# Attention and a non-local block on one core: a third score block at the start of each attention, the bias of the values in one accumulator slot, an ordered first load with products of zeros ahead of it, and the last chunk of z in halves

## The chip, the cores and the metric

The kernel runs on one core of a Trainium2 chip. The metric is the device time in microseconds (us), from the first to the last instruction of that core; smaller is better. Before the change three runs took 2209.11, 2209.64 and 2211.08 us; the median is 2209.64 us. The profile shown is one execution with a span of 2209.6 us.

The engines are TensorE (PE in the profile; PEld is its loading of weights), VectorE (DVE), ScalarE (ACT), GpSimd (POOL) and SyncE (SP). DMA transfers are issued here from the SP and the ACT queue, and all use the core's 16 DMA engines.

## The reference

Eight images of 512 channels and 32 x 32 positions, float32. Cut to what is computed:

```python
def layer0(x, Wq, bq, Wk, bk, Wv, bv, Wp, bp):          # 8 heads of 64 channels
    q, k, v = conv1x1(x, Wq, bq), conv1x1(x, Wk, bk), conv1x1(x, Wv, bv)
    attn = softmax(einsum('bhdn,bhdm->bhnm', q, k) * 64 ** -0.5)
    return x + conv1x1(einsum('bhnm,bhdm->bhdn', attn, v), Wp, bp)

def layer1(x, g_w, g_b, theta_w, theta_b, phi_w, phi_b, W_w, W_b, gamma, beta):
    g, theta, phi = conv1x1(x, g_w, g_b), conv1x1(x, theta_w, theta_b), conv1x1(x, phi_w, phi_b)
    f = einsum('bcn,bdn->bcd', theta, phi) / n
    z = conv1x1(einsum('bcd,bdn->bcn', f, g), W_w, W_b) + x
    mean, var = z.mean((0, 2, 3)), z.var((0, 2, 3))      # over all eight images
    return (z - mean) * rsqrt(var + 1e-5) * gamma + beta

out = layer1(layer0(x))
```

The normalization at the end needs the statistics of a channel over all eight images, so no output can be stored before the last image's z of that channel is there.

## The kernel before

PSUM, where TensorE writes, is cut into four slots of two banks each. A list `free` holds their names from the one idle longest to the one used last. `next_bank` takes the one idle longest.

```python
    free = ["s0", "s1", "s2", "s3"]

    def bank(tag, name):
        return psum.tile([P, 2, 512], F32, tag=tag, name=name)

    def next_bank(name):
        free.append(free.pop(0))
        return bank(free[-1], name)
```

The large products (q, k, v, the projection, theta and phi, g, z) are each done as seven products of quarter matrices instead of eight. The quarters of a weight are loaded as `w[:, 0]`, `w[:, 1]`, `w[:, 2]` and a corner `a21`; four sums of them, `w[:, 3]` to `w[:, 6]`, are made by VectorE, as are four sums of the quarters of the data (`t1` to `t4`). Three slots take the products; the fourth of the list stands idle during them, and the slot used last goes to the end of the list.

```python
    def weight_sums(w, a21):
        for to, l, r, op in ((3, a21, w[:, 2], ALU.add), (4, w[:, 3], w[:, 0], ALU.subtract),
                             (5, w[:, 0], a21, ALU.subtract), (6, w[:, 1], w[:, 4], ALU.subtract)):
            nc.vector.tensor_tensor(w[:, to], l, r, op)
    ...
    # (name, weight, data, slot, quarters of the result that read the slot after it)
    SEVEN = (("11", 0, "11", 0, (("11", True),)), ("s1t1", 3, "t1", 1, (("22", True),)),
             ("s2t2", 4, "t2", 0, (("12", True),)), ("s4", 6, "22", 1, (("12", False),)),
             ("s3t3", 5, "t3", 0, (("22", False),)), ("12", 1, "21", 2, (("11", False),)),
             ("t4", 2, "t4", 0, (("21", True),)))
    EARLY = (SEVEN[0], SEVEN[5], *SEVEN[1:4], ...)        # the order for q of image 0

    def seven(name, w, data, positions_out, first, add, between=None, early=False):
        nk, half = w.shape[2], w.shape[3]
        tags = list(free)
        free[:] = [tags[3], tags[1], tags[0], tags[2]] if early else [tags[3], tags[1], tags[2], tags[0]]
        ...
            for to_ps, at, lhsT, rhs in parts:
                for k in range(nk):
                    pe(nc.tensor.matmul(to_ps, lhsT(k), rhs(k), start=(s, at) not in begun, stop=(k == nk - 1),
                                        skip_group_check=True))
                    begun.add((s, at))
            for to, is_first in reads:
                (first if is_first else add)(to, ps)
```

The first loads: four of the first weight on the ACT queue, four of the first image on the SP queue, then two small biases and the second weight.

```python
    load_w(nc.scalar)
    for h in range(NH):
        for k in range(2):
            at = slice(k * CC // 2, (k + 1) * CC // 2), slice(h * 512, (h + 1) * 512)
            nc.sync.dma_start(xt[:, at[0], at[1]], x_v[0, :, at[0], at[1]])
    bq, bk = load_col("bq", nc.scalar), load_col("bk", nc.scalar)
    load_w(nc.sync)
    ...
    data = data_sums(quarters_of(xt), "x_0")
    q, peak_q = heads_of(0, "q", weights("WqT"), bq, data, early=True)
```

The attention of one image has 64 steps. A step makes a block of scores in a slot, takes the exponential on ScalarE, and two steps later (`LAG`) multiplies it with the values. Two slots alternate for scores, two for the weighted sums of one unit of eight steps and the next.

```python
        def scores(i):
            u, m = steps[i]
            ps = bank(tags[i % 2], f"ps_{b}_{u}_{m}")
            ...                                            # four matmuls
            e = block(f"e_{b}_{u}_{m}")
            nc.scalar.activation(e, ps, AF.Exp, scale=SCALE)
            ...                                            # sums of e on VectorE

        def weighted(i):
            u, m = steps[i]
            if m == 0:
                sums[u] = bank(tags[2 + u % 2], f"po_{b}_{u}")
            ...                                            # four matmuls, at the end two reads
        ...
        for i in range(len(steps) + LAG):
            if i < len(steps):
                scores(i)
            if i >= LAG:
                weighted(i - LAG)
```

The bias of the values goes through the projection into the projection's bias, once, before the projection of image 0:

```python
    def join_bias(w):
        for oc in range(CC):
            m, mc = divmod(oc, CC // 2)
            ps = next_bank(f"pbp_{oc}")
            for c in range(CC):
                ...
                pe(nc.tensor.matmul(ps[:, 0, :1], quarter[:, kc, mc * P:(mc + 1) * P], bv[:, c:c + 1],
                                    start=(c == 0), stop=(c == CC - 1)))
            nc.vector.tensor_tensor(bp[:, oc:oc + 1], bp[:, oc:oc + 1], ps[:, 0, :1], ALU.add)
```

The end: z of the last three images, one chunk of 128 channels (`oc`) after the other. After the third image of a chunk the statistics of that chunk are joined (`begin`), its factors computed and all eight images of the chunk scaled and stored (`finish`).

```python
    def last_z():
        order = [B - LATE, B - 1, *range(B - LATE + 1, B - 1)]
        begun = None
        for oc in range(CC):
            for n, b in enumerate(order):
                _, g, wf = late[b]
                ps = next_bank(f"pz_{b}_{oc}")
                for h in range(NH):
                    for d in range(IC):
                        pe(nc.tensor.matmul(ps[:, h, :], wf[:, d, oc * P:(oc + 1) * P], g[d][:, h * 512:(h + 1) * 512],
                                            start=(d == 0), stop=(d == IC - 1)))
                t = z[b][oc]
                dve(nc.vector.scalar_tensor_tensor(t, ps.rearrange("p h n -> p (h n)"), wb[:, oc:oc + 1], t,
                                                   ALU.add, ALU.add))
                if n == 0 and begun:
                    finish(oc - 1, *begun)
                for h in range(NH):
                    dve(nc.vector.bn_stats(stats[:, oc, b * NH + h, :], t[:, h * 512:(h + 1) * 512]))
            begun = begin(oc)
        finish(CC - 1, *begun)
```

`pe(...)` and `dve(...)` keep the instructions so marked in the order of the program on their engine; the others may be moved by the scheduler.

Of the kernel before, what the change touches and what calls it, by code (L numbers as in the profile page):

```python
# [8 lines left out]
F32 = mybir.dt.float32  # L9
# [21 lines left out]
def unshifted(ctx: ExitStack, tc: tile.TileContext, a: dict, out: bass.AP):  # L31
# [11 lines left out]
    LATE = 3  # L43
    LAG = 2
# [86 lines left out]
    def weights(name):  # L131

        n, w = loaded.pop(0)
        assert n == name
        if name not in kept:
            weight_sums(w, corner[name])
            kept[name] = dram.tile(list(w.shape), F32, tag=f"kept_{name}", name=f"kept_{name}")
            nc.sync.dma_start(kept[name], w)
        return w

    def join_bias(w):

        for oc in range(CC):
            m, mc = divmod(oc, CC // 2)
            ps = next_bank(f"pbp_{oc}")
            for c in range(CC):
                k, kc = divmod(c, CC // 2)
                quarter = {(0, 0): w[:, 0], (0, 1): w[:, 1], (1, 0): corner["WpT"], (1, 1): w[:, 2]}[m, k]
                pe(nc.tensor.matmul(ps[:, 0, :1], quarter[:, kc, mc * P:(mc + 1) * P], bv[:, c:c + 1],
                                    start=(c == 0), stop=(c == CC - 1)))  # L150
            nc.vector.tensor_tensor(bp[:, oc:oc + 1], bp[:, oc:oc + 1], ps[:, 0, :1], ALU.add)  # L151
# [23 lines left out]
    def seven(name, w, data, positions_out, first, add, between=None, early=False):  # L175
# [7 lines left out]
        for n, (what, wi, di, s, reads) in enumerate(EARLY if early else SEVEN):  # L183
# [11 lines left out]
            for to_ps, at, lhsT, rhs in parts:  # L195
                for k in range(nk):
                    pe(nc.tensor.matmul(to_ps, lhsT(k), rhs(k), start=(s, at) not in begun, stop=(k == nk - 1),  # L197
                                        skip_group_check=True))
                    begun.add((s, at))
# [19 lines left out]
    load_w(nc.scalar)  # L219
    for h in range(NH):  # L220
        for k in range(2):
            at = slice(k * CC // 2, (k + 1) * CC // 2), slice(h * 512, (h + 1) * 512)
            nc.sync.dma_start(xt[:, at[0], at[1]], x_v[0, :, at[0], at[1]])
# [27 lines left out]
    def heads_of(b, what, w, bias, data, **how):  # L251
# [13 lines left out]
        for c in range(CC):  # L265
            nc.vector.tensor_reduce(peak[:, c:c + 1], t[:, c, :], AX.X, ALU.max, apply_absolute_value=True)
# [30 lines left out]
    def attention(b, q, k, v, near_end):  # L297
# [18 lines left out]
        def scores(i):  # L316
            u, m = steps[i]
            p, h = units[u]
            ps = bank(tags[i % 2], f"ps_{b}_{u}_{m}")
# [216 lines left out]
# [3 lines that stand above are left out]
        for oc in range(CC):  # L539
            for n, b in enumerate(order):  # L540
                _, g, wf = late[b]
                ps = next_bank(f"pz_{b}_{oc}")
                for h in range(NH):
                    for d in range(IC):
                        pe(nc.tensor.matmul(ps[:, h, :], wf[:, d, oc * P:(oc + 1) * P], g[d][:, h * 512:(h + 1) * 512],  # L545
                                            start=(d == 0), stop=(d == IC - 1)))
# [320 lines left out]
```

## Time and profile before

| What | Value |
|---|---|
| Time, median of three runs | 2209.64 us |
| Span of the profiled execution | 2209.6 us |
| PE busy | 2166.6 us (98%) |
| DVE busy | 1321.1 us (60%) |
| ACT busy | 735.8 us (33%) |
| First matmul of image 0 | at 6.29 us |
| First score block of image 0 | at 81.7 us |
| Last large matmul ends | at about 2187.5 us |
| First store of the output issued | at 2162.75 us |
| Moved by DMA over the span | 209.07 MB |

How to read the lines: a row of the waits has the engine and line that waited, what it waited for, then the total in us, how often and the longest. A row of the timeline has the start and the length in us, the engine, the line of the kernel, the operation, what is written and what is read, their shapes and how many instructions were merged; in brackets stands the idle time ahead of it and what ended it. One float32 matmul of the program appears as two passes, each with its weight load.

### The profile page before, as it was taken

Reading aid. Unit: us, or ns where it says so; the run is one execution under the profiler, and the core shown is the slowest. Engines: PE = TensorE matmul, PEld = TensorE weight load, DVE = VectorE, ACT = ScalarE, POOL = GpSimd, SP = SyncE. Lnnn points to the kernel's source line nnn. Section 1 sums busy time; section 2 is a strip of 40 time slices with the busy share of each in tenths; the row PEclk is TensorE's granted clock in tenths of the full one; section 3 lists DMA queues with packets and bytes.
Section 4 is the critical chain, followed back from the end, with each engine's and each line's share of the span. In section 5 each row is a group of like instructions: output and inputs, shape, how many; then the busy total and the mean of one; then the engine's idle time right before and its main releaser. Section 6 shows DMA issues by size and latency. Waiting matters only on the chain.

```text
span 2209.6 us, 28905 instructions
## 1 busy us (share of the span) xinstructions
PE 2166.6 (98%) x12234; PEld 1066.1 (48%) x12234; DVE 1321.1 (60%) x1299; ACT 735.8 (33%) x821; POOL 35.4 (2%) x36
## 2 busy tenths in 40 slices
PE   8999999999999999999999999999999999999996
PEld 3534664346633456335563365633655336643362
DVE  5476546765467644776547755467463765447736
ACT  1463103641046310462105621165203641055215
POOL 0000000000000000000000000000000000000000
PEclk9999999999999999999999999999999999999998
DMA  6212323113131232312223113231334113222347
GB/s 238 77 39 60 126 98 120 39 44 133 60 129 39 60 107 75 116 40 69 96 93 105 40 64 119 90 91 31 108 114 143 39 30 129 79 84 66 129 159 306
DMA packets 58265, 209.07 MB, mean 95 GB/s; under 512 B 10384, under 2 KB 16784, under 8 KB 52752
## 3 DMA queue, kind: packets, MB, share of 16 engines
q1 hardware_dynamic: 56752, 206.09, 28.5%
q8 instruction: 98, 1.61, 0.3%
q10 hardware_dynamic: 1376, 1.05, 0.2%
q14 instruction: 39, 0.32, 0.0%
HBM read 129.12 MB, written 46.53 MB: 79 GB/s over the span
## 4 chain that ended last, share of the span: by engine, by line
PE 93%; DMA 3%; DVE 2%; issue 1%; ACT 1%; SPq 0%; DVEq 0%; ACTq 0%
PE ps L324 19%; PE po L346 19%; PE pp L197 9%; PE pq L197 9%; PE ptp L197 9%; PE pv L197 8%; PE pk L197 6%; PE pg L197 4%; PE pf L449 3%; PE pz L197 2%; DMA r<-den_d 2%; PE pz L545 2%; PE pwf L468 1%; PE den L295 1%; ACT e L327 0%
## 5 line engine op out<-in xcount | busy, mean ns | idle before, releaser
L327 ACT ACTIVATE e<-ps 128x1024 f32<-128x1024 f32 x512 | 523.7, 1024 | 390.7 <-PE ps L324 383.1
L333 DVE TENSOR_TENSOR acc<-acc,e 128x1024 f32<-128x1024 f32 x384 | 470.0, 1224 | 123.7 <-ACT e L327 117.1
L324 PE MATMUL ps<-q,k 64*64 64x512 f32 x4096 | 532.4, 591 | 2.6 <-ACT e L327 2.6
L346 PE MATMUL po<-e,v 64*64 64x512 f32 x4096 | 529.5, 590 | 0.0
L324 PEld LDWEIGHTS ps<-q,k 64*64 64x64 f32 x4096 | 155.0, 133 | 291.6 <-issue 278.9
L346 PEld LDWEIGHTS po<-e,v 64*64 64x64 f32 x4096 | 156.7, 133 | 283.9 <-issue 281.2
L458 ACT ACTIVATE g<-pg,gb 128x512 f32<-128x512 f32 x32 | 22.0, 687 | 434.3 <-PE pg L197 434.3
L331 DVE TENSOR_TENSOR acc<-e,e 128x1024 f32<-128x1024 f32 x64 | 78.2, 1223 | 121.0 <-ACT e L327 87.7
L197 PE MATMUL pk<-t_x,w_WkT 128*128 128x512 f32 x256 | 114.0, 593 | 0.7 <-DVE k L214 0.7
L197 PE MATMUL pv<-w_WvT,t_x 128*128 128x256 f32 x512 | 114.5, 379 | 0.0
L197 PE MATMUL ptp<-w_tp,t_x 128*128 128x256 f32 x512 | 114.4, 379 | 0.0
L197 PE MATMUL pp<-t_o,w_WpT 128*128 128x512 f32 x256 | 113.7, 593 | 0.0
L197 PE MATMUL pq<-t_x,w_WqT 128*128 128x512 f32 x256 | 113.6, 592 | 0.0
L197 PEld LDWEIGHTS ptp<-w_tp,t_x 128*128 128x128 f32 x512 | 97.3, 190 | 13.2
L197 PEld LDWEIGHTS pv<-w_WvT,t_x 128*128 128x128 f32 x512 | 97.2, 190 | 13.2
L197 PE MATMUL pq<-x,w_WqT 128*128 128x512 f32 x192 | 89.7, 612 | 6.3 <-DMA w_WqT<-in_WqT_dram 6.3
L262 ACT ACTIVATE k<-pk,bk 128x512 f32<-128x512 f32 x64 | 40.5, 684 | 165.0 <-PE pk L197 165.0
L384 DVE TENSOR_TENSOR o<-o,r 128x512 f32<-128x512 f32 x60 | 40.8, 689 | 91.0 <-DMA r<-den_d 91.0
L197 PE MATMUL pp<-o,w_WpT 128*128 128x512 f32 x192 | 91.1, 620 | 2.2 <-DVE bp L151 2.2
L278 ACT COPY v<-pv 128x1024 f32<-128x1024 f32 x32 | 32.4, 1012 | 173.6 <-PE pv L197 173.6
L262 ACT ACTIVATE q<-pq,bq 128x512 f32<-128x512 f32 x62 | 39.2, 683 | 146.2 <-PE pq L197 146.2
L197 PE MATMUL pv<-w_WvT,x 128*128 128x256 f32 x384 | 87.5, 381 | 0.0
(132 smaller groups left out, 1947.4 us busy)
## 6 DMA issues: line engine op xcount, KB each, us to landing
fold<-acc SPq DMA_DIRECT2D x240, 128.0 KB, 2.3
x<-in_x_dram SPq DMA_DIRECT2D x32, 512.0 KB, 5.5
r<-den_d SPq DMA_DIRECT2D x120, 128.0 KB, 3.0
w_WqT<-kept_WqT SPq DMA_DIRECT2D x7, 1792.0 KB, 7.4
w_WvT<-kept_WvT SPq DMA_DIRECT2D x7, 1792.0 KB, 7.3
w_WkT<-kept_WkT SPq DMA_DIRECT2D x7, 1792.0 KB, 7.1
w_WpT<-kept_WpT SPq DMA_DIRECT2D x7, 1792.0 KB, 8.7
w_tp<-kept_tp SPq DMA_DIRECT2D x7, 1792.0 KB, 7.3
```

Source lines behind the costliest of these rows:

```text
L197: pe(nc.tensor.matmul(to_ps, lhsT(k), rhs(k), start=(s, at) not in begun, stop=(k == nk - 1), skip_group_check=True))
L262: nc.scalar.activation(t[:, c, cols(q)], ps[:, m, :], AF.Identity, bias=bias[:, c:c + 1])
L278: seven(f"pv_{b}", w, data, True, lambda q, ps: nc.scalar.copy(at(q), as_v(ps)), lambda q, ps: nc.vector.tensor_tensor(at(q), at(q), as_v( ...
L295: pe(nc.tensor.matmul(ps[j * D:(j + 1) * D, :], lhsT, rhs(j), start=True, stop=True, skip_group_check=True))
L324: pe(nc.tensor.matmul(ps[c * P // 2:(c + 1) * P // 2, j, :], k[r, p, keys], q[r, p, h * 512:(h + 1) * 512], start=True, stop=True, skip_gr ...
L327: nc.scalar.activation(e, ps, AF.Exp, scale=SCALE)
L331: nc.vector.tensor_tensor(accs[u], es[u, 0], e, ALU.add)
L333: nc.vector.tensor_tensor(accs[u], accs[u], e, ALU.add)
L346: pe(nc.tensor.matmul(ps[j * D:(j + 1) * D, r, :], v[keys, m, (2 * p + j) * D:(2 * p + j + 1) * D], e[keys, j, :], start=(m == 0), stop=(m ...
L384: dve(nc.vector.tensor_tensor(part(4 * g + i), part(4 * g + i), r, ALU.mult))
L449: pe(nc.tensor.matmul(ps[:, c, :], tp[:, i, c * P:(c + 1) * P], tp[:, i, CI:], start=(i == 0), stop=(i == NB - 1)))
L545: pe(nc.tensor.matmul(ps[:, h, :], wf[:, d, oc * P:(oc + 1) * P], g[d][:, h * 512:(h + 1) * 512], start=(d == 0), stop=(d == IC - 1)))
```

## The change

It has four parts. In an attention the third score block (step 2) goes to a slot that is not needed before the second unit, so three blocks can be made before the first exponential is done; the two slots then alternate the other way round. The four columns of the joined bias go into one slot and are added by one instruction. At the start the loads of the first image and of the first weight are issued in pairs, smallest first, eight products of zeros run on TensorE ahead of the first real one, the first product goes through its channels chunk by chunk, and the sums of data and weights are put in one order. The last chunk of z is made, added and counted in halves.

```diff
+    WARM = 8
...
     def join_bias(w):
 
+        ps = next_bank("pbp")[:, 0, :CC]
         for oc in range(CC):
             m, mc = divmod(oc, CC // 2)
-            ps = next_bank(f"pbp_{oc}")
             for c in range(CC):
...
-                pe(nc.tensor.matmul(ps[:, 0, :1], quarter[:, kc, mc * P:(mc + 1) * P], bv[:, c:c + 1],
-                                    start=(c == 0), stop=(c == CC - 1)))
-            nc.vector.tensor_tensor(bp[:, oc:oc + 1], bp[:, oc:oc + 1], ps[:, 0, :1], ALU.add)
+                pe(nc.tensor.matmul(ps[:, oc:oc + 1], quarter[:, kc, mc * P:(mc + 1) * P], bv[:, c:c + 1],
+                                    start=(c == 0), stop=(c == CC - 1), skip_group_check=True))
+        nc.vector.tensor_tensor(bp, bp, ps, ALU.add)
...
-            for to_ps, at, lhsT, rhs in parts:
-                for k in range(nk):
-                    pe(nc.tensor.matmul(...))
+            work = [(*part, k) for part in parts for k in range(nk)]
+            if by_chunk and n == 0:
+                work.sort(key=lambda one: one[4])
+            for to_ps, at, lhsT, rhs, k in work:
+                pe(nc.tensor.matmul(...))
...
-    load_w(nc.scalar)
-    for h in range(NH):
-        for k in range(2):
-            at = slice(k * CC // 2, (k + 1) * CC // 2), slice(h * 512, (h + 1) * 512)
-            nc.sync.dma_start(xt[:, at[0], at[1]], x_v[0, :, at[0], at[1]])
+    warm = const.tile([P, P], F32, tag="warm", name="warm")
+    nc.vector.memset(warm, 0.0)
+    w_first = wr.tile([P, 7, 2, C // 2], F32, tag="w", name="w_WqT")
+    loaded.append((queue.pop(0), w_first))
+    corner["WqT"] = block("a21_WqT")[:, :, :C // 2]
+    for x_part, w_part in (((0, 1, 0), (w_first[:, 0], 0, 0, 0, 1)), ((1, 2, 0), (w_first[:, 0], 0, 0, 1, 2)),
+                           ((2, 4, 0), (w_first[:, 1], 0, 1, 0, 2)), ((0, 2, 1), (w_first[:, 2], 1, 1, 0, 2)),
+                           ((2, 4, 1), (corner["WqT"], 1, 0, 0, 2))):
+        c0, c1, h = x_part
+        at = slice(h * 512, (h + 1) * 512)
+        nc.sync.dma_start(xt[:, c0:c1, at], x_v[0, :, c0:c1, at])
+        to, m, k, c0, c1 = w_part
+        nc.scalar.dma_start(to[:, c0:c1], quarter("WqT", m, k)[:, c0:c1])
+    ps = next_bank("warm_ps")[:, 0, :]
+    for i in range(WARM):
+        pe(nc.tensor.matmul(ps[:, :P], warm, warm, start=True, stop=True))
...
-            nc.vector.tensor_reduce(peak[:, c:c + 1], t[:, c, :], AX.X, ALU.max, apply_absolute_value=True)
+            ins = nc.vector.tensor_reduce(peak[:, c:c + 1], t[:, c, :], AX.X, ALU.max, apply_absolute_value=True)
+            if b == 0:
+                dve(ins)
...
-            ps = bank(tags[i % 2], f"ps_{b}_{u}_{m}")
+            ps = bank(tags[(0, 1, 3)[i] if i < 3 else (i + 1) % 2], f"ps_{b}_{u}_{m}")
...
                 t = z[b][oc]
-                dve(nc.vector.scalar_tensor_tensor(t, ...))
...
+                halves = ((0, 1), (1, 2)) if (oc, n) == (CC - 1, LATE - 1) else ((0, NH),)
+                for h0, h1 in halves:
+                    ps = next_bank(f"pz_{b}_{oc}_{h0}")[:, :h1 - h0, :]
+                    ...                                    # the matmuls, the sum and the statistics of h0 to h1
...
-    data = data_sums(quarters_of(xt), "x_0")
-    q, peak_q = heads_of(0, "q", weights("WqT"), bq, data, early=True)
+    b11, b12, b21, b22 = quarters_of(xt)
+    t = [block(f"t{i}_x_0") for i in range(4)]
+    w, a21 = w_first, corner["WqT"]
+    for to, l, r, op in ((t[0], b12, b11, ALU.subtract), (w[:, 3], a21, w[:, 2], ALU.add),
+                         (w[:, 4], w[:, 3], w[:, 0], ALU.subtract), (t[1], b22, t[0], ALU.subtract),
+                         (w[:, 6], w[:, 1], w[:, 4], ALU.subtract), (t[2], b22, b12, ALU.subtract),
+                         (w[:, 5], w[:, 0], a21, ALU.subtract), (t[3], b21, t[1], ALU.subtract)):
+        dve(nc.vector.tensor_tensor(to, l, r, op))
+    data = {"11": b11, "21": b21, "22": b22, "t1": t[0], "t2": t[1], "t3": t[2], "t4": t[3]}
+    q, peak_q = heads_of(0, "q", weights("WqT", True), bq, data, early=True, by_chunk=True)
```

## The prediction

> **What bounds the kernel now.** I read the page's busy shares first, because they decide what kind of gain is possible at all:
>
> ```profile
> PE 2166.6 (98%) x12234; PEld 1066.1 (48%) x12234; DVE 1321.1 (60%) x1299; ACT 735.8 (33%) x821; POOL 35.4 (2%) x36
> ```
>
> TensorE (PE) is busy in 2166.6 of 2209.6 us. The change removes no large product, so it can only win in the 43 us in which PE stands idle, or where PE runs slowly. About 22 us of the 43 lie after the last matmul (2187.7 to 2209.6). The rest is in the table of waits, for PE alone (us in total, times, longest):
>
> ```profile
> PE pq L197 <- DMA w_WqT<-in_WqT_dram: 6.3, 1, 6.3
> PE psum L295 <- DVE acc L333: 4.9, 1, 4.9
> PE psum L295 <- DVE ri L373: 3.8, 1, 3.8
> PE ps L324 <- ACT e L327: 2.6, 8, 0.3
> PE pp L197 <- DVE bp L151: 2.2, 1, 2.2
> PE pk L197 <- DVE k L214: 0.7, 2, 0.5
> ```
>
> Four parts of the change aim at the first, fourth and fifth row and at the tail. The two psum waits (last image) are not touched. So I then read the timeline at those four places. The start:
>
> ```profile
> 6.29 0.50 PEld L197 LDWEIGHTS pq<-x,w_WqT 128*128 128x128 f32 x2 [6.29 <-DMA w_WqT<-in_WqT_dram]
> 11.57 0.34 PEld L197 LDWEIGHTS pq<-x,w_WqT 128*128 128x128 f32 x1 [0.52 <-issue]
> 12.17 0.19 PEld L197 LDWEIGHTS pq<-x,w_WqT 128*128 128x128 f32 x1 [0.26 <-DMA w_WkT<-in_WkT_dram]
> 16.03 7.03 PE L197 MATMUL pq<-t_x,w_WqT 128*128 128x512 f32 x16
> ...
> 11.29 0.69 DVE L108 TENSOR_TENSOR w_WqT<-a_WqT,w_WqT 128x512 f32<-128x512 f32 x1 [9.44 <-DMA a_WqT<-in_WqT_dram]
> 13.83 1.22 DVE L157 TENSOR_TENSOR t_x<-x 128x1024 f32<-128x1024 f32 x1
> ```
>
> PE starts at 6.29. Until 11.57 a weight load takes 0.34 us and the passes follow each other every 0.86 us; from 12.17 on it is 0.19 us and 0.43 us. An fp32 product of 512 columns is two such passes. The first two products of q ("11" and "12", 16 passes) therefore take 16.03 - 6.29 = 9.74 us instead of 16 x 0.43 = 6.88. Then the beginning of an attention, and where its third score block stands:
>
> ```profile
> 81.72 1.95 PE L324 MATMUL ps<-q,k 64*64 64x512 f32 x16
> 82.88 1.94 ACT L327 ACTIVATE e<-ps 128x1024 f32<-128x1024 f32 x2
> 83.95 1.09 PE L324 MATMUL ps<-q,k 64*64 64x512 f32 x8 [0.28 <-ACT e L327]
> ```
>
> A score block (8 passes) takes half of the 1.716 us between one block of a kind and the next in the steady loop (84.86, 86.58, 88.30 for the weighted sums), 0.858 us. The third one waits until the first exponential has emptied its slot. The bias of the values:
>
> ```profile
> 267.84 4.59 DVE L266 TENSOR_REDUCE peak_k<-k 128x1 f32<-128x1024 f32 x4
> 269.72 0.58 PE L149 MATMUL pbp<-bvc,w_WpT 128*128 128x1 f32 x4
> 272.34 0.34 DVE L151 TENSOR_TENSOR bp<-bp,pbp 128x1 f32<-128x1 f32 x4
> 272.54 6.46 PE L197 MATMUL pp<-o,w_WpT 128*128 128x512 f32 x8 [2.24 <-DVE bp L151]
> ```
>
> PE has finished the small products at about 270.3, but all four slots are taken by them, and VectorE (DVE) empties them only after four reductions. Last the tail, as a DVE row and two rows of the table of stretches (PE, PEld, DVE, ACT, POOL busy, granted clock, DMA share, GB/s):
>
> ```profile
> 2187.54 1.28 DVE L548 SCALAR_TENSOR_TENSOR x<-pz,Wb,x 128x1024 f32<-128x1024 f32 x1 [0.51 <-PE pz L545]
> ...
> 2175.00:2180.00 5.00, 5.00 (x13) 2.17 (x12) 4.38 (x7) 5.00 (x5) 0.00 (x0) 1.00 1.02 405
> 2200.00:2202.00 2.00, 0.00 (x0) 0.00 (x0) 0.00 (x0) 0.00 (x0) 0.00 (x0) 0.50 1.02 391
> ```
>
> The DMA engines are full (share 1.02, about 400 GB/s) from 2165 to 2204 without a break: the stores of the output are a backlog, and the chain of waits, which follows PE, DVE and ACT into the tail, doesn't show that.
>
> **What the Trainium skill says.** "TensorE: Matmul & The Clock Gate", section "Part 1: The HAM clock gate", says the array starts at half clock and is released by about 3.4 us of sustained work, measured in a free-running window. The trace agrees in kind: half speed (0.86 against 0.43 us a pass) for 5.3 to 5.9 us after the first matmul, which is one full window plus part of another. The page's granted clock, 1.00 throughout the start, doesn't show it. The same section puts the floor between two short matmuls at about 25 ns; here 32 passes of one column, each with a weight load of its own, follow each other every 0.11 us (3.6 us from 266.67), so I take the measured 0.11 us for a pass of 128 columns, and twice that when cold. "DMA: Bandwidth & Descriptors", section "Queues, rings and completion order", says each engine takes packets in turn from the queues it has work for, and consumes a queue's descriptors in ring order. If so, pairing an x load on one queue with a weight load on the other, smallest first, makes pairs land in order. The trace before fits: landing order follows issue order on each queue. "PSUM — Partial Sum Buffer", Specifications, gives 8 banks of 2 KiB; the four slots of two banks in this kernel are all of it, so a third score block needs a slot that is idle anyway.
>
> **The start.** From the table of stretches, summed by microsecond, 0.15 MB had moved by 3 us, 0.49 by 4, 0.80 by 5, 1.19 by 6, 1.58 by 7, 1.98 by 8, 2.35 by 9, 3.05 by 11. The first x (512 KB) and weight load (256 KB), 0.79 MB, were landed at 6.06 and 6.25, so a landing comes 1.1 to 1.8 us after its last byte. In the new order the pairs end at 0.39, 0.79, 1.57, 2.36 and 3.15 MB, hence land at about 5.0, 6.2, 8.2 to 8.8, 10.4 and (x, a21) 11.3 to 12.7. Eight loads were issued before the ninth waited for a first landing (the fourth x at 6.09, bk at 6.27), so the fifth pair is issued at about 5.0; its bytes are not due before 9.0, so that costs nothing.
>
> The 8 zero products (16 passes of 128 columns, 0.22 us cold) run from about 1.0 to 4.7 us, on zeros that DVE makes at 0.85. The clock should be full somewhere between 4.5 and 7.9. Product "11" runs by chunks: chunk 0 from 5.0, chunk 1 from 6.2 to 6.7, to about 8.5. "12" waits for pair three and ends at 8.8 + 8 x 0.43 = 12.2. The third product needs t1 (from b12 and b11: ready by 11.7) and w3 (a21 landed, plus 0.69): 12.0 to 13.4. I take 12.6. It was 16.03, so **3.4 us** are won. Of this 2.9 is the cold time of 9.74 - 6.88, and the rest the earlier beginning; the loads then bind. Nothing later takes it back: k's weights are summed by 22.2 and needed at 33.4, the values' by 40.4 and needed at 57.4. The first read of "11" by ACT needs bq, a table load (1.28) and 2 x 0.63 us, until about 15.3; its slot is wanted again at 12.6 + 3.4 = 16.0, which is close.
>
> **The third score block.** Without the wait it starts 1.716 us after the first. It starts 83.95 - 81.79 = 2.16 after it in image 0, 360.98 - 358.82 = 2.16 in image 1, and 1947.43 - 1945.22 = 2.21 in the last two. That is 6 x 0.44 + 2 x 0.49 = **3.6 us**. The slot it takes held the product read last before the attention. It is free in time: image 0, copy to 82.84 against 83.51; image 6, copy of wf to 1689.15 against 1690.24; the closest is image 1, where DVE reads 1.39 us from 358.96, to 360.35, against 360.54. Afterwards PE sets the pace (1.716 us a step, ACT 1.02, DVE 1.23), so nothing returns as a wait.
>
> **The bias in one slot.** Same 32 passes, same end at 270.3; the projection starts then, in the next slot, which is long free: **2.2 us**. DVE adds the bias in one instruction of about 0.16 us instead of four. The next possible wait: DVE must read product "11" before the third product at 270.3 + 6.9 = 277.2. It has reductions to 272.4, sums of the tp weights to about 275.4, then two reads of 0.7, to 276.8. It just holds.
>
> **The last chunk by halves.** Before, statistics ended at 2190.15. DVE is busy with the chunk before until 2187.03, so halves only fill its 0.51 us of idleness: some 0.4 to 0.5 us earlier for the last factors. But the stores stand in a backlog of full DMA engines and end when they end: **0**.
>
> **Sum.** 3.4 + 3.6 + 2.2 + 0 = 9.2 us, and 2209.64 - 9.2 = 2200.4 us. All stores and reloads at the end stand relative to PE's work and move with it.
>
> **Rivals.** (1) The start is bound by its bytes and the clock doesn't come early: zero products too weak to count as activity, or a gap before the first real one. Then "11" and "12" stay partly cold, and only 1 to 1.5 us of 3.4 remain: 2202.6. For it: the two kinds of wait lie close together, both near 12.5. Against it: the passes are dense. (2) A read of PSUM takes the wait's place: DVE in images 1 to 5 (margin 0.19 us), the tp sums at 276.8, bq at 15.3. Each could cost 0.2 to 1 us: 2201.5. (3) The loads arrive faster since they are ordered, a21 at about 11: 4.5 us at the start, 2199.3. (4) The halves do shorten the end, if the stores were not a backlog: 0.5 more, 2199.9. The DMA share of 1.02 speaks against it.
>
> **Range and chances.** The scores and the bias are differences of two rows and sure to some tenths; the start is sure to about 1.5 us; three runs before spread over 2.0 us. So 2198.5 to 2203.0. Two per cent is 44 us, five times what PE's idle time at these places holds: within 2% is all but certain.
>
> **What would show it.** PE's waits: the eight on ACT e gone, the one on bp gone, the first wait split into short ones that end near 12.5, and the first product with t_x at 12.6 instead of 16.03; the third score block 1.72 us after the first in every image; the projection 3.6 us after the bias products begin; DMA share still 1.02 to the end, with last statistics to last landing no shorter than before. I'd be wrong if the third block waits for DVE, if weight loads of 0.34 us are still seen after 8 us, or if the span falls by under 6 or over 12 us.

## The result and the profile after

The changed kernel takes 2200.45 us (median of six runs, 2200.11 to 2202.75) against 2209.38 us for the kernel before in the same series (six runs, 2207.88 to 2211.08). The ratio is 0.9961, with a 95% interval from 0.9948 to 0.9974: 8.9 us less. Predicted were 2200.4 us.

| What | Before | After |
|---|---|---|
| Span of the profiled execution | 2209.6 us | 2198.7 us |
| First product on t1 begins | 16.03 us | 13.03 us |
| First score block of image 0 | 81.72 us | 78.82 us |
| Bias products begin | 266.67 us | 263.26 us |
| Projection of image 0 begins | 272.54 us | 266.75 us |
| Last z begins | 2146.13 us | 2135.58 us |
| From there to the end of the span | 63.4 us | 63.1 us |

The page's first part and the table of waits of TensorE, of the changed kernel (engine, line that waited, what it waited for: total us, times, longest):

```profile
PE 2164.0 (98%) x12250; PEld 1067.6 (49%) x12250; DVE 1320.5 (60%) x1298; ACT 734.8 (33%) x821; POOL 35.4 (2%) x36
```

```profile
PE psum L313 <- DVE acc L351: 4.8, 1, 4.8
PE psum L313 <- DVE ri L391: 3.8, 1, 3.8
PE pk L202 <- DVE k L219: 1.6, 2, 1.4
PE pq L202 <- DVE w_WqT L606: 1.3, 1, 1.3
PE warm_ps L239 <- DVE warm L225: 1.1, 1, 1.1
```

The eight waits on ACT, the one on bp and the 6.3 us on the first load are gone. One wait has grown, that of the k product on VectorE's read (0.7 before, 1.6 now). The two large waits of the last image stand as they were. The start, from the timeline (start, length, engine, line, what is written and read, and in brackets the idle time ahead and what ended it):

```profile
1.06 3.66 PE L239 MATMUL warm_ps<-warm 128*128 128x128 f32 x16 [1.06 <-DVE warm L225]
4.56 7.18 PE L202 MATMUL pq<-x,w_WqT 128*128 128x512 f32 x16
...
11.15 1.23 DVE L606 TENSOR_TENSOR t_x<-x 128x1024 f32<-128x1024 f32 x1 [9.15 <-DMA x<-in_x_dram]
12.29 0.68 DVE L606 TENSOR_TENSOR w_WqT<-a_WqT,w_WqT 128x512 f32<-128x512 f32 x1
13.03 7.13 PE L202 MATMUL pq<-t_x,w_WqT 128*128 128x512 f32 x16 [1.28 <-DVE w_WqT L606]
```

TensorE now does "11" and "12" while the loads arrive and then waits 1.28 us for the sum w3, which VectorE makes right after t1. The attention of image 0:

```profile
78.82 2.81 PE L342 MATMUL ps<-q,k 64*64 64x512 f32 x24
79.98 2.86 ACT L345 ACTIVATE e<-ps 128x1024 f32<-128x1024 f32 x3
```

One row now holds 24 passes, three score blocks without a gap. And the bias of the values:

```profile
263.26 1.84 PE L151 MATMUL pbp<-bvc,w_WpT 128*128 128x1 f32 x16
...
266.30 0.58 PE L151 MATMUL pbp<-bvc,w_WpT 128*128 128x1 f32 x4
266.75 5.38 PE L202 MATMUL pp<-o,w_WpT 128*128 128x512 f32 x8
269.25 0.15 DVE L153 TENSOR_TENSOR bp<-bp,pbp 128x4 f32<-128x4 f32 x1
```

The projection follows the small products at once, 3.5 us after they begin (5.9 before), and VectorE's one addition comes 2.5 us later, when nobody waits for it. But look at the third row: its eight passes take 5.21 us, counted from their start to the start of the next product at 271.96 (a row's own length, 5.38, runs to the end of its last pass, which overlaps the next row). At full clock they take 3.44 to 3.52. Nobody waits there; TensorE is slow. That is what the prediction had overlooked. The tail, from the table of stretches (PE, PEld, DVE, ACT, POOL busy, granted clock, DMA share, GB/s):

```profile
2175.00:2180.00 5.00, 2.15 (x7) 0.76 (x5) 4.79 (x10) 5.00 (x6) 0.00 (x0) 1.00 1.03 406
...
2190.00:2195.00 5.00, 0.00 (x0) 0.00 (x0) 0.00 (x0) 0.00 (x0) 0.00 (x0) 0.50 0.94 375
```

The DMA engines are full until about 2194 us (the last stretch holds their end), as they were until 2204 before.

How the difference builds up along the two traces, read at the same product of each: 3.0 us earlier at the first product on t1, 2.9 at the first scores, 3.4 after image 0's attention, 5.8 when the projection begins and 6.9 at its second product, 7.4 at q of image 2, then 6.2 at its scores (1.2 given back, where k's product waits), 7.3 at image 5, 8.9 at image 7 and 10.6 at the last z. The two profiled spans differ by 10.9 us, more than the medians (8.9); part of that is the clock at the bias, as will be seen.

### The profile page after: what moved, and what is told of

It is laid out like the page before. It is cut to its first block, busy times and chain, and to the rows that moved or that the text cites. A ratio compares the mean times of both kernels' runs of the same rounds, so it can differ in the third digit from the quotient of the medians.

```text
span 2198.7 us, 28934 instructions
## 1 busy us (share of the span) xinstructions
PE 2164.0 (98%) x12250; PEld 1067.6 (49%) x12250; DVE 1320.5 (60%) x1298; ACT 734.8 (33%) x821; POOL 35.4 (2%) x36
## 4 chain that ended last, share of the span: by engine, by line
PE 94%; DMA 2%; DVE 2%; ACT 1%; issue 1%; SPq 0%; ACTq 0%; DVEq 0%
PE ps L342 20%; PE po L364 20%; PE pp L202 9%; PE ptp L202 9%; PE pv L202 9%; PE pq L202 9%; PE pk L202 7%; PE pg L202 4%; PE pf L467 3%; PE pz L202 2%; DMA r<-den_d 2%; PE pz L566 2%; PE pwf L486 1%; PE den L313 1%; DVE acc L351 0%
```

## The experiments

The theory from the prediction: the parts are independent and worth about 3.4 us (start, 2.9 of it from the clock), 3.6 (scores), 2.2 (bias) and 0 (halves). The rivals: the start is bound by loads and by the order of VectorE's sums and not by the clock; a wait on VectorE or ScalarE takes the place of one removed; and, formed only after the trace, a block of one-column products lets TensorE's clock fall whatever it waits for. Medians are compared with those of the kernel before in the same series: 2207.99 us (46 runs) for the first four, 2208.97 (9) for the next four, 2209.94 (11) for the last four. In brackets stands the 95% interval of the ratio; 0.001 of it is 2.2 us, so the medians alone tell parts of this size apart only roughly.

### Each part alone, on the kernel before

**The third score block alone.**

```diff
-            ps = bank(tags[i % 2], f"ps_{b}_{u}_{m}")
+            ps = bank(tags[(0, 1, 3)[i] if i < 3 else (i + 1) % 2], f"ps_{b}_{u}_{m}")
```

> The kernel before with the third score block in the idle slot, nothing else. Theory (each image saves the stall between second and third block, 0.51 us in images 0 to 5 and 0.56 in 6 and 7 by the two traces): 4.2 us less, about 2205.2 us; third block 1.72 us after the first in all eight images, no wait of PE for ACT e. Rival (the gain is given back where the normalization's transfers or VectorE hold PE later in the image): 2 us or less, 2207.4 us or more, with longer waits of pk for DVE k.

Measured: 2203.54 us, ratio 0.9979 [0.9970, 0.9987], 4.45 us less. No wait on ACT is left in its table. It is the largest of the four parts. In the trace of the whole change an attention, from its first scores to the next image's first product of q, takes 110.03 us in every image. In the kernel before it took 110.54 in images 0 and 1 and 110.59 in images 2 to 6. So 0.51 us are saved in two images and 0.56 in the other six (for image 7 by the spacing of its blocks), 4.4 us together, which is what this run shows. The expectation had the two figures, but six images of the first kind and two of the second.

**The bias in one slot alone.**

```diff
+        ps = next_bank("pbp")[:, 0, :CC]
         for oc in range(CC):
-            ps = next_bank(f"pbp_{oc}")
...
-            nc.vector.tensor_tensor(bp[:, oc:oc + 1], bp[:, oc:oc + 1], ps[:, 0, :1], ALU.add)
+        nc.vector.tensor_tensor(bp, bp, ps, ALU.add)
```

> The kernel before with the four columns of the joined bias in one slot, nothing else. Theory (the wait of 2.24 us falls away, and the clock, which has dropped during the small products, comes back earlier): projection starts 3.6 us after the first bias product instead of 5.9, and its first product (8 passes) takes about 5.2 us instead of 6.3, together 3.4 us less, about 2206.0 us. Rival (as predicted: only the wait): first product still 6.3 us, 2.2 us less, 2207.2 us.

Measured: 2205.51 us, ratio 0.9990 [0.9983, 0.9997], 2.48 us less. The interval, 0.7 to 3.8 us, holds both expected gains, 3.4 and 2.2. The projection begins 3.49 us after the bias products, as expected. In this one profile the clock did not fall: the first eight passes of the projection took 3.52 us, not 5.2 or 6.3. This run also happened to tell of the start, which is here the old one. Its timeline:

```profile
6.11 8.86 PE L197 MATMUL pq<-x,w_WqT 128*128 128x512 f32 x16 [6.11 <-DMA w_WqT<-in_WqT_dram]
...
15.49 1.22 DVE L157 TENSOR_TENSOR t_x<-x 128x1024 f32<-128x1024 f32 x1
16.77 7.13 PE L197 MATMUL pq<-t_x,w_WqT 128*128 128x512 f32 x16 [1.80 <-DVE t_x L157]
```

The clock was full at 9.61 us in this execution, against 11.90 in the profile shown for the kernel before. Yet the first product on t1 came no earlier: TensorE stood for 1.80 us and waited for t1, which VectorE makes only at 15.49, behind four sums of weights, the first of which waits until the corner a21 has landed (12.95). The other two runs with the old start, the scores alone and the halves alone, show the same wait (0.7 and 1.3 us; the product at 16.52 and 16.66). Only in the profile shown in front was TensorE the later one, and there t1 was done at 15.05, 1 us before the product at 16.03.

**The start alone.** The changed kernel's loads in pairs, products of zeros, chunk order and order of the sums; scores, bias and z as before.

```diff
+    WARM = 8
...
+    for x_part, w_part in (((0, 1, 0), (w_first[:, 0], 0, 0, 0, 1)), ...):
...
+    for i in range(WARM):
+        pe(nc.tensor.matmul(ps[:, :P], warm, warm, start=True, stop=True))
...
+    for to, l, r, op in ((t[0], b12, b11, ALU.subtract), (w[:, 3], a21, w[:, 2], ALU.add), ...):
+        dve(nc.vector.tensor_tensor(to, l, r, op))
```

> The kernel before with the new start alone (paired loads, zero products, first product by chunks, sums in one order). Theory: first product on t1 at about 13.0 us instead of 16.03, k starts 2.9 us earlier, 2206.5 us. Rival (the clock's window falls differently from run to run, so the full clock at 4.4 us was luck): weight loads of 0.34 us after 4.5 us and a gain of only 1 to 2.5 us.

Measured: 2205.97 us, ratio 0.9990 [0.9982, 0.9998], only 2.02 us less; the interval, 0.4 to 4.0 us, holds both expectations. At its own place the gain is there: the first product on t1 begins at 12.83, against 16.03 to 16.77 in the four traces with the old start. From its table of waits:

```profile
PE pp L202 <- DVE bp L153: 2.5, 1, 2.5
PE pk L202 <- DVE k L219: 1.0, 2, 0.8
```

Compared with the next run, whose start is the old one, it is 3.8 us earlier when the bias products begin (263.58 against 267.41), 2.6 at the projection (269.72 against 272.33) and 1.7 at the scores of image 2 (624.64 against 626.31). But these are two single executions. Against the profile of the kernel before (266.67, 272.54 and 627.62 at the same places) it is 3.1, 2.8 and 3.0 us earlier. Up to image 2, then, 2.2 us of the gain are given back by the one comparison and 0.2 by the other; the places are the bias, where VectorE's reductions and the clock both have a hand in it, and k of image 2, which waits for VectorE.

**The last chunk by halves alone.**

```diff
+                halves = ((0, 1), (1, 2)) if (oc, n) == (CC - 1, LATE - 1) else ((0, NH),)
+                for h0, h1 in halves:
+                    ps = next_bank(f"pz_{b}_{oc}_{h0}")[:, :h1 - h0, :]
...                                        # the matmuls, the sum and the statistics of h0 to h1
```

> The kernel before with the last chunk of z by halves, nothing else. Theory (stores are a backlog of full DMA engines): last statistics 0.5 us earlier, end of the stores unchanged, 2209.4 us within 0.3. Rival (the chain of waits through statistics and factors sets the end): 0.5 us less, 2208.9 us.

Measured: 2207.97 us, ratio 0.9999 [0.9990, 1.0007]: nothing that can be told, though an interval of 2.2 us less to 1.5 us more would hide the 0.5 us of the rival. Its table of stretches, near the end:

```profile
2190.00:2195.00 5.00, 0.00 (x0) 0.00 (x0) 0.44 (x1) 2.09 (x2) 0.00 (x0) 0.50 1.03 401
```

The compute engines are nearly done and the DMA engines still move 401 GB/s. From the beginning of the last z the last statistics end after 43.73 us with halves and after 44.01 without, 0.28 us earlier. The end of the span comes after 63.42 us here; the four traces without halves have 63.26 to 63.75, the nine others with halves 63.10 to 63.26. So this run shows no gain, and all traces together do not exclude one of 0.3 us.

The four parts together: 4.45 + 2.48 + 2.02 + 0.02 = 8.97 us. The whole change gave 8.93. Each part is uncertain by 1.5 to 2 us to either side, so an agreement as close as this is partly luck; what it shows is that no large gain or loss is hidden in their combination.

### What the start and the bias rest on, edits of the changed kernel

**No products of zeros.**

```diff
-    WARM = 8
+    WARM = 0
```

> The changed kernel without the eight zero products. Theory (the zeros only bring the full clock forward; a cold stretch of 3.4 to 6.8 us would cost 1.7 to 3.4 us, of which about 2 us are waited for loads anyway, 0.7 ahead of the second product and 1.3 ahead of the third): first product on t1 at 13.0 to 14.4 us, total 0 to 1.4 us above the changed kernel. Rival (the zeros are the whole gain of the start): back at 16 us, 2.9 us above it.

Measured: 2199.31 us, ratio 0.9956 [0.9942, 0.9969], the same as with them. Two views of its timeline, TensorE and VectorE:

```profile
4.34 9.05 PE L202 MATMUL pq<-x,w_WqT 128*128 128x512 f32 x16 [4.34 <-DMA w_WqT<-in_WqT_dram]
...
13.23 7.04 PE L202 MATMUL pq<-t_x,w_WqT 128*128 128x512 f32 x16
```

```profile
10.70 1.23 DVE L602 TENSOR_TENSOR t_x<-x 128x1024 f32<-128x1024 f32 x1 [8.84 <-DMA x<-in_x_dram]
11.84 0.69 DVE L602 TENSOR_TENSOR w_WqT<-a_WqT,w_WqT 128x512 f32<-128x512 f32 x1
```

"11" and "12" now run partly at half clock, up to 8.24 us, and take 9 us; the product on t1 still begins at 13.23, 0.2 us later than in the first trace with the zeros. The loads landed earlier here, though: w3 is done at 12.53, so in this execution the slow passes cost 0.7 us. The zeros do release the clock: over the nine traces with them it was full 3.1 to 6.0 us after the first one (in five of these the first real passes were still slow). By these traces they buy 0.2 to 0.7 us of some 3, for most of the slow passes lie beside the loads and the wait for w3, and the medians show none of it.

**The bias with 128 columns.** The same 32 passes, but the moving operand is each bias column spread over 128 columns. Four small VectorE operations more make it, and four additions read it. Nothing of the computation is left out.

```diff
-        ps = next_bank("pbp")[:, 0, :CC]
+        ps = next_bank("pbp")[:, 0, :]
...
-                pe(nc.tensor.matmul(ps[:, oc:oc + 1], quarter[:, kc, mc * P:(mc + 1) * P], bv[:, c:c + 1],
+                pe(nc.tensor.matmul(ps[:, oc * P:(oc + 1) * P], quarter[:, kc, mc * P:(mc + 1) * P],
+                                    wide[:, c // 2, (c % 2) * P:(c % 2 + 1) * P],
```

> The changed kernel with each product of the joined bias streaming 128 equal columns instead of one (same 32 passes and weight loads, four more small reads and four sums). Theory (one-column products count as idleness for the clock): 32 passes still take 3.5 us, granted clock stays 1.00, first product of the projection 3.4 to 3.7 us instead of 5.2; 0 to 1.8 us less than the changed kernel, by where the clock's window fell. Rival (the clock falls for another reason, a switch of shapes or the weight loads): 0.50 is seen again in two or more of the windows after the bias.

Measured: 2198.53 us, ratio 0.9951 [0.9938, 0.9965]. The timeline and one stretch of this kernel:

```profile
262.93 1.95 PE L155 MATMUL pbp<-bv_wide,w_WpT 128*128 128x128 f32 x16
...
266.05 0.61 PE L155 MATMUL pbp<-bv_wide,w_WpT 128*128 128x128 f32 x4
266.50 3.60 PE L208 MATMUL pp<-o,w_WpT 128*128 128x512 f32 x8
```

```profile
266.00:270.00 4.00, 4.00 (x15) 2.09 (x15) 4.00 (x10) 0.00 (x0) 0.00 (x0) 1.00 0.20 69
```

The 32 passes last as long as before (3.57 us; 3.49 with one column), the granted clock stays at 1.00, and the projection's first eight passes take 3.44 us to the start of the next product. Beside it the same stretch of the changed kernel, and one of the kernel before:

```profile
266.00:270.00 4.00, 4.00 (x13) 2.21 (x14) 4.00 (x6) 0.00 (x0) 0.00 (x0) 0.66 0.35 104
```

```profile
274.00:278.00 4.00, 4.00 (x6) 1.52 (x5) 1.26 (x2) 0.00 (x0) 0.00 (x0) 0.50 0.55 229
```

TensorE is shown busy for all 4.00 us in each, but the clock is at 0.66 and 0.50. In the kernel before, TensorE waited 2.24 us there, so one could lay the drop to the wait. In the changed kernel there is no wait, and it drops all the same.

One trace of the wide form is thin evidence, since one trace of the narrow form (the bias in one slot alone) shows no drop either. The mean clock of whole runs supports it: it was 0.993 or 0.994 in all five runs with the wide bias, and 0.992 in eight of the ten runs of the two kernels of the same series with the one-column block (no zeros, w3 first).

**The bias spread over k of image 1.** The products of one output column are done after each of four products of k.

```diff
-    def join_bias(w):
+    def join_bias(w, oc, joined={}):
...
-            k, peak_k = heads_of(b + 1, "k", weights("WkT"), bk, nxt["data"])
+                how["between"] = {n: lambda oc=oc: join_bias(w, oc) for oc, n in enumerate((3, 4, 5, 6))}
+            k, peak_k = heads_of(b + 1, "k", wk, bk, nxt["data"], **how)
```

> The changed kernel with the four columns of the joined bias put between the last four products of k of image 1 (0.9 us each) instead of in one block of 3.5 us. Theory: no stretch of low activity is as long as a window of 3.4 us, the clock stays at 1.00 through 280 us in every run, and the first product of the projection takes 3.4 us; 0 to 1.8 us less than the changed kernel. Rival (activity is counted in sum): 0.50 again somewhere between 250 and 275 us.

Measured: 2197.98 us, ratio 0.9947 [0.9933, 0.9960]. Its timeline:

```profile
261.98 3.68 PE L204 MATMUL pk<-t_x,w_WkT 128*128 128x512 f32 x8
265.49 0.50 PE L152 MATMUL pbp<-bvc,a_WpT 128*128 128x1 f32 x4
...
266.30 3.68 PE L204 MATMUL pp<-o,w_WpT 128*128 128x512 f32 x8
```

Still one column each, but eight at a time between dense products: the clock stays full until 2017 us. The durations of the projection's first eight passes, to the start of the next product, over all traces sort the causes. With the small products as one block in one slot: 3.52, 5.21, 5.21, 6.28 and 6.42 us. As a block in four slots: 6.30, 6.38, 5.56 and 5.71. Widened: 3.44. Spread: 3.52, 3.51, 3.52 and 3.52. A block is followed by a slow product in eight of nine traces, the other two forms in none of five. In the run with the halves alone the drop can be seen to begin inside the block: four small passes take 0.58 us at its start and 0.99 at its end, with no wait between.

**w3 ahead of t1.** VectorE's first two sums exchanged, since w3's operands land first.

```diff
-    for to, l, r, op in ((t[0], b12, b11, ALU.subtract), (w[:, 3], a21, w[:, 2], ALU.add),
+    for to, l, r, op in ((w[:, 3], a21, w[:, 2], ALU.add), (t[0], b12, b11, ALU.subtract),
```

> The changed kernel with the weight sum w3 ahead of the data sum t1 on VectorE. Theory (a21 has landed at 10.1 us, b12 at 11.1, so w3 costs nothing while b12 is awaited): first product on t1 at 12.4 us instead of 13.03, 0.6 us less. Rival (a21's landing is late in other runs and then holds t1): no gain.

Measured: 2200.22 us, ratio 0.9958 [0.9945, 0.9972]: no gain that can be told. Its first product on t1 begins at 12.08 instead of 13.03, so the step is right at its place. But its profile has the slowest first product of the projection (6.42 us), and the execution of the next run, without this exchange, began the product on t1 at 12.21. Arrivals differ by more than this edit is worth.

### The changed kernel again, and further than it

**The changed kernel once more,** to see how far its bias differs from one execution to the next. It has no edit.

> The changed kernel once more, unaltered, on the chip of the next three. Theory of the clock's window: the same program loses 0, 1.7 or 3.4 us at the projection of image 0 by where the window falls, so the first product of the projection takes between 3.4 and 6.6 us, not always the 5.2 us of the first trace; total 2198.5 to 2202.8 us. Rival (the 5.2 us belong to the program): 5.2 us again.

Measured: 2198.93 us, the median of five runs, ratio 0.9955 [0.9942, 0.9968]; a sixth, in which the clock was 0.555 and the time 3868.73 us, is left out. The same code, another profile, and below it one more stretch of the first profile:

```profile
262.00:266.00 4.00, 4.00 (x32) 3.75 (x30) 4.00 (x5) 1.27 (x2) 0.00 (x0) 0.91 0.51 155
266.00:270.00 4.00, 4.00 (x8) 2.02 (x8) 3.01 (x5) 0.00 (x0) 0.00 (x0) 0.50 0.14 41
270.00:274.00 4.00, 4.00 (x8) 1.77 (x7) 0.99 (x2) 0.00 (x0) 0.00 (x0) 0.74 0.00 0
```

```profile
270.00:274.00 4.00, 4.00 (x9) 1.68 (x9) 1.97 (x4) 0.00 (x0) 0.00 (x0) 0.91 0.00 0
```

Half clock throughout this stretch, where the first profile had 0.66. Summing the stretches from 262 to 274 us, (1 - granted clock) x 2 x 4 us gives 0.34 and 0.09 x 8 = 3.4 us at half clock in the first profile, and 0.09, 0.50 and 0.26 x 8 = 6.8 us in this one: once and twice 3.4 us.

Why once here and twice there can be worked out from the traces. In each trace every drop and every return of the granted clock lies on one grid of 3.41 us (267.29 and 270.71 in the first profile, 265.29 and 272.11 in this one), and the grid lies differently in each execution. Count how much of one window of the grid the small products fill, with the wait behind them if there is one. In the eight traces with a drop it was 74 to 100% of the window that ended where the clock fell. In the one block without a drop (the bias in one slot alone) it was 44% of one window and 58% of the next. The wide block filled at most 67% of a window, which is why its single trace decides little, and a group of the spread form lasts 0.8 us. Where the next window was dense throughout, the clock came back after 3.41 us (two traces); where 1.0 us or more of it was still small products or waiting, it stayed at half for 6.83 us (six traces).

**Bias spread and w3 ahead, together.** Both edits as shown above.

```diff
+    for to, l, r, op in ((w[:, 3], a21, w[:, 2], ALU.add), (t[0], b12, b11, ALU.subtract),
```

> The changed kernel with both small edits, the bias spread between the products of k and w3 ahead of t1. Theory: they add, 0.7 us at the start and 0 to 3.4 us at the bias (about 1.7 in the mean), 2.4 us under the changed kernel, about 2198.0 us; no 0.50 of the clock before 2000 us. Rival (the start's gain is lost to the later waits of k for VectorE): as the spread bias alone, 0.7 us more.

Measured: 2197.04 us, ratio 0.9944 [0.9931, 0.9956], 1.9 us under the changed kernel in the same series, where 2.4 were expected. The two intervals overlap, so this step is likely but not settled. The product on t1 begins at 11.84, the projection's first passes take 3.51 us.

**The first denominators of the last image earlier.** They are summed at step 38 instead of 46, in a slot of their own.

```diff
+            if alone and i == 38:
+                d = denominators(0, bank(tags[3], "den_38")[:, 0, :])
...
-                if i == 46:
-                    d = denominators(0, ps[:, 1, :])
```

> The same, and in the last image the four units' denominators at step 38 in a slot of their own instead of at step 46 in a slot shared with unit 4's. Theory: the wait of psum for DVE ri (3.8 us) goes, and with it the clock's fall at 2018 us (0.50 for 3.4 or 6.8 us, worth 1.7 to 3.4 us); 5 to 7 us less than without it, about 2192 us. Rival (the wait only moves: the reciprocal of 3.35 us at step 38 holds VectorE's sums and then PE): a wait of 2 us or more at 2000 to 2010 us, 2 us or less won.

Measured: 2193.04 us, ratio 0.9926 [0.9913, 0.9939], 4.0 us less than the version before it, less than I had expected; each of its runs is below each of that version. One line of the waits of that version, then one of this:

```profile
PE psum L315 <- DVE ri L393: 3.8, 1, 3.8
```

```profile
PE po L366 <- DVE ri L393: 0.6, 1, 0.6
```

The wait on `ri` falls from 3.8 to 0.6 us, and with it goes a drop of the clock at 2018 us (3.41 us long), which the version before it still shows. By the two profiles the last image, from its first scores to the last z, is 4.7 us shorter.

**The last image's products of o and r on GpSimd.**

```diff
+                if alone:
+                    nc.gpsimd.tensor_tensor(part(4 * g + i), part(4 * g + i), r, ALU.mult)
+                else:
+                    dve(nc.vector.tensor_tensor(part(4 * g + i), part(4 * g + i), r, ALU.mult))
```

> The same, and the four normalizing products of the last image's first half on GpSimd instead of VectorE. Theory (VectorE has a backlog ahead of the last sum, and PE waits 4.8 us for it): the last wait of psum falls to 2 us or less, 2 to 4 us less than without it, about 2189 us. Rival (GpSimd is slow, or it and VectorE hold each other up at SBUF): no gain, or a new wait for POOL.

Measured: 2189.07 us, ratio 0.9912 [0.9899, 0.9924], again 4.0 us less, and again each run is below each of the version before it. Its waits:

```profile
PE psum L315 <- DVE acc L353: 2.2, 1, 2.2
...
PE po L366 <- DVE ri L393: 0.5, 1, 0.5
```

The wait on `acc` falls from 4.8 to 2.2 us, which fits VectorE, rid of four products, getting to the sums of e sooner. That is 2.6 of the 4.0 us. The two profiles differ by 1.4 us already at the first scores of the last image (1933.83 and 1932.39), ahead of all that this edit touches, so by them the edit itself is worth about 3. GpSimd takes 1.27 to 1.99 us for a 128x512 product that VectorE does in 0.69; TensorE's table has no wait for it. This version is 20.9 us under the kernel before and 9.9 under the changed one.

## Why the prediction was right, and where it was not

The time and the sum came out; the terms did not all do so. Predicted against measured with each part alone: 3.4 against 2.02 (start), 3.6 against 4.45 (scores), 2.2 against 2.48 (bias), 0 against 0.02 (halves). The errors of -1.4, +0.9 and +0.3 cancel. With 1.5 to 2 us of uncertainty on each, the medians alone would not show that a term was wrong; the traces do, and they say where. That the sum came out so closely is luck in part.

**The start: the place was right, its cause and its end were not.** 12.6 was predicted for the product on t1, with 12.0 to 13.4 as its range; 13.03 and 12.21 were measured. The step that failed is "Of this 2.9 is the cold time": without the zeros 0.2 to 0.7 us are lost, not 2.9. The kernel without zeros has slow passes until 8.24 us and begins the product at 13.23; the run with the bias alone had a faster clock and the old order, and began at 16.77. A full clock alone could have won 1 us in the profile that I read (t1 done at 15.05, the product at 16.03), and nothing in the other three. What carries the gain is the order of loads and sums: the first real product begins at 4.34 to 4.72 instead of 6.04 to 6.29, and t1 and w3 are made from 11.15 to 12.97, where the old order began t1 at 13.83 to 15.49. The loads and the sums were not tried apart. In the four traces with the old start TensorE was done with "11" and "12" at 14.97 to 16.03, so an estimate from its waits for t1 is that the order of the sums alone could have won 0 to 1.8 us. The prediction said of the new start that clock and loads lie close together; I had not asked the same of the old one, where VectorE's order stood right behind the clock. The Trainium skill, "TensorE: Matmul & The Clock Gate", section "Part 1: The HAM clock gate", names 3413 ns for the window and calls it free-running; the traces agree: the grid of 3.41 us found at the bias, carried back to the start, has lines at 11.90 (kernel before), 9.61 (bias alone), 8.24 (no zeros) and 4.46 (changed kernel), and there the passes become fast.

The second step that failed is "Nothing later takes it back". In the whole change the bias takes nothing back, since its wait is gone, but 1.2 us go at k of image 2: VectorE waits 2.09 us there for the transfer of a normalization (`r<-den_d`), and so reads k only at 533.15, 20.9 us after k begins. In the kernel before it waited 1.79 us at the same place, but read k 19.7 us after its beginning. TensorE's wait for VectorE's reads of k was 0 to 0.7 us in the four traces with the old start, 0.2 in the one without zeros, and 0.9 to 2.6 in the others. Why it grows when the start moves was not tried and stays open.

**The scores: right mechanism, a size too small.** I set the new spacing at two blocks of the steady loop and got 0.44 and 0.49 us an image; the traces show 0.51 and 0.56. Most of this is that a block after a wait costs more than 0.858 us: in image 0 before, the third block began at 83.95 and the next product at 84.86, 0.91 us later. The rest of the term is a miscount: the larger stall is not that of "the last two" images but of six, for in image 2 the third block began at 629.83 and the first at 627.62, 2.21 us apart already. With 2 x 0.51 + 6 x 0.56 the term is 4.4. The closest margin, image 1, held: VectorE reads from 352.08 to 353.47, the weights of the third block are loaded from 353.53, and it begins at 353.63, 1.77 us after the first as in every image; no wait on VectorE is in the table for it.

**The bias: right, with a term missing.** The wait of 2.24 us is gone and the run with this part alone gives 2.48. I read the 32 small passes as work, for the profile shows TensorE busy, and did not look at the clock behind them. It falls to half for one or two windows of 3.4 us after a block of one-column passes in eight of nine traces, before the change and after it, and that costs 1.8 us (5.21 against 3.44) to 3.0 us (6.42) in the first product alone. The spread form doesn't have it in four traces, nor the wide one in its one. In the mean of the traces that product takes 5.99 us with four slots and 5.33 with one, so the clock may have added some 0.7 us to the gain of this part; it did make the two profiled spans differ by 1.1 us more (6.30 against 5.21 us), part of the 2 us by which they differ more than the medians.

**The halves: right as far as it can be told.** VectorE's statistics end 0.28 us earlier (0.4 to 0.5 were predicted); that the stores end earlier is not shown, and the traces leave room for 0.3 us at most.

Of the rivals, (1) fell in an unforeseen way: the zeros do wake the clock, and it matters little. (2) did not occur at the places named, but at another, k of image 2. (3) came half: a21 landed at about 10.1 us, but b12 only at 11.15, and w3 stands behind t1 on VectorE, so the gain did not grow to 4.5. (4) was not seen; 0.5 us of it is more than the traces allow.

## What to carry to other kernels

A block of very small matmuls can let TensorE's clock fall as a wait does, even where the profile shows the engine busy (here 3.5 us of one-column products, half clock in eight of nine traces), so spread it between dense products, and read the granted clock behind every such block. At the very start read the length of the passes instead: the granted clock stood at 1.00 there while they took 0.86 us in place of 0.43. Order first loads and the sums made from them by when their operands land, and ask of each wait that is to be removed which one stands right behind it: zeros ahead of a start that is bound by loads bought at most 0.7 us, and a shorter chain ahead of stores that fill the DMA engines nothing that could be told. After a change that moved 9 us, the waits that nobody had touched were worth as much: two edits in the last image brought 8 us.

## What was not expected of the hardware

- 32 one-column passes, 3.5 us with TensorE shown busy without a gap, are followed, or already cut into, by half clock in eight of nine traces, for 3.41 us in two and 6.83 us in six; the same passes in groups of eight between dense products are not in four traces. 32 passes of 128 columns that last as long (3.57 us) are not in one trace, which the clocks of its other runs support. Whether the block drops the clock, and for how long, goes with its place on a grid of 3.41 us: it did where it filled 74% or more of one window, and did not at 58%.
- Products of zeros release the clock like others: 3.1 to 6.0 us after the first, over nine traces; real ones took 3.5 to 5.6 us in the five traces without zeros.
- A product of 128x512 float32 elements took 1.27 to 1.99 us on GpSimd in the last image, and 0.69 us on VectorE.
